# Reordering the lead-in of an attention and feed-forward layer: Q's half rows, the parts' buffers, and V as pieces

## The chip, the core and the metric

The kernel runs on one core of a Trainium2 chip. A core has TensorE (PE, matrix products from SBUF into PSUM), VectorE (DVE), ScalarE (ACT), GpSimd (POOL) and SyncE (SP), which run side by side and wait for each other by semaphores; transfers between HBM and SBUF are issued by an engine's queue (here SP and ACT) and carried by 16 shared DMA engines. The metric is the device time of one execution in microseconds (us), lower is better. Each engine executes its own instructions in the order in which they are written.

## What is computed

One post-norm transformer layer on x of 8 batches x 1024 rows x 256. Attention has 16 heads of width 16 with a fixed additive mask on the distance between query and key; the feed-forward part has ternary weights with a scale and a low-rank addition. Cut to what matters here:

```python
Q = split_heads(x @ Wq.T + bq)
K = split_heads(x @ Wk.T + bk)
V = split_heads(x @ Wv.T + bv)
scores = einsum('bhqd,bhkd->bhqk', Q, K) / sqrt(16)
scores = scores + prior_lambda * gaussian_mask(1024)
attn = softmax(scores, axis=-1)
out = einsum('bhqk,bhkd->bhqd', attn, V)       # heads put together again
x = layernorm(x + out @ Wo.T + bo)
x = layernorm(x + ffn(x))                      # ternary weights, relu squared, low rank
```

## The kernel before

**Parts.** A product in full precision is made of several in a rounded type: Q and K are split into a rounded copy and the rounded difference, and both are kept as the two halves of a tile two. For a chunk of 8 heads (128 rows of Q or K) write_parts (line 190) writes them to HBM in an order of four 16-row layers per head, with two DMAs for K and three for Q per half of 512 columns. fill_stack (line 287) reads them back, four tiles for K and four for Q per group G of 4 heads, as operands stack["k", ...] and stack["q", ...] with 64 rows of layers, 256 KB each. The stack has two slots, so group G + 1 is filled while G is worked on.

**Two passes over the scores.** For every block of 128 queries max_scores (line 636) multiplies Q by K, and max_row (line 658) adds the mask and takes the maximum over 1024 keys in one VectorE instruction of about 1.22 us, whose elementwise result goes to a tile with the tag junk that nobody reads. set_max (line 672) turns the 16 x 128 maxima of one half, negates and splits them, writes them to HBM and reads them back as two extra rows of stack["q"]. exp_scores (line 699) then computes the transposed scores with those rows, so the maximum is subtracted by the product itself; ACT takes the exponential, and weigh (line 749) multiplies by V and by a column of ones.

**The loop.** The loop at line 1462 counts g from -12 (LEAD) to the end. In step g the maxima of item g + 12 are computed and, from g = 0 on, the exponentials of item g; one item is a pair of 128x1024 score blocks for 2 heads. So steps -12 to -1 are the lead-in: maxima alone. PSUM in the loop is three score tiles (se, used in turn), one accumulator (av), and two half banks (misc, used in turn) for everything else. That else is a list of pieces, jobs: products of Q and K for the other 8 heads and for the next batch, turning of x, V, the feed-forward part. A piece issues its matmuls and returns a second function that empties the half bank. In the lead-in, every second step takes one piece from jobs (two at g = -12): the load of x(1, 0) and six of the eight pieces of queries_keys(0, 1).

**Before the loop.** SP loads x's half 0, the biases of K and Q, x's half 1, lambda and bv; ACT issues the loads of the four weights. PE turns the weights and x (128 x 128 transposes), first_part (line 199) makes parts of K half 0, Q half 0, K half 1 and Q half 1 for the first 8 heads. In each, ACT reads the product from PSUM twice (a full copy and the rounded one), VectorE subtracts, and the lower 64 rows (the first 4 heads) are written to HBM at once; the writes of the upper 64 rows are kept in second_heads. Then fill_stack(0) is issued with K on SP's queue and Q on ACT's (line 301), then second_heads, then fill_stack(1) (line 327) and five small loads. Between, PE computes V of batch 0 with 32 records (line 317) and VectorE adds its bias (line 307). The tiles two have the tags two, junk, o0 and o1: buffers that later work uses for other things.

**Order.** At the end of the function all instructions of an engine are chained in written order, so a late operand holds up whatever stands behind it on that engine. A tile that takes over a tag waits until the last reader of the old tile, DMAs included, is done. DMA completions are counted on eight semaphores in rotation, so a DMA also waits for the one issued eight before.

Of the kernel before, what the change touches and what calls it, by code (L numbers as in the profile page):

```python
# [16 lines left out]
P = 128  # L17
HD = 16
# [20 lines left out]
def tile_postln_layer(  # L39
# [60 lines left out]
        x_of[b, half] = t  # L100

    load_x(0, 0)
    raw = {}
    for name, w in (("k", wk), ("q", wq), ("v", wv), ("o", wo)):
        t = big(f"raw_{name}")[:, : NDC * D].rearrange("p (c d) -> p c d", d=D)
# [3 lines left out]
    for name, src in (("k", bk), ("q", bq)):  # L109
        t = cpool.tile([P, NDC], F32, tag=f"b{name}", name=f"b{name}")  # L110
        nc.sync.dma_start(t, src.rearrange("(c p) -> p c", p=P))
        bcol[name] = t
    load_x(0, 1, "hi")
    lam = cpool.tile([P, 1], F32, tag="lam", name="lam")
    nc.sync.dma_start(lam, prior_lambda.partition_broadcast(P))
    bv_row = cpool.tile([P, D], F32, tag="bv_row", name="bv_row")
# [35 lines left out]


    qscale = float(HD) ** -0.5
    nc.vector.tensor_scalar_mul(bcol["q"], bcol["q"], qscale)
    wT = {}

    def turn_weights(name, copy):

        t = cpool.tile([P, NDC, D], F32, tag=f"w{name}T", name=f"w{name}T")  # L160
        pt = bank0(f"pt_{name}")
        for dc in range(NDC):
            for ec in range(NDC):
                at = NDC * dc + ec
                nc.tensor.transpose(pt[:, ts(at, P)], raw[name][:, ec, ts(dc, P)], ident)
        copy(t.rearrange("p c d -> p (c d)"), pt)
        wT[name] = t


    xT = cpool.tile([P, NDC, L], F32, tag="xT", name="xT")  # L170
# [2 lines left out]
    def first_turn(half):  # L173
        xb = x_of.pop((0, half))
        for dc in range(NDC):
            pt = bank0(f"ptx_0_{dc}_{half}")
            for c in range(QB):
                nc.tensor.transpose(pt[:, ts(c, P)], xb[:, c, ts(dc, P)], ident)
            nc.scalar.copy(xT[:, dc, ts(half, HALF)], pt)
        turned[0, half] = 2 * NDC  # L180

    parts_of, made = {}, {}
# [13 lines left out]
            nc.sync.dma_start(to[:, 2, :], two[:, 1, :])  # L196
            nc.sync.dma_start(to[:, 3, :], two[:, 0, :])

    def first_part(name, scale, half, tag, full):
        pt = bank0(f"p{name}_0_0_{half}")  # L200
        for dc in range(NDC):
            nc.tensor.matmul(
                pt,
                wT[name][:, dc, :P],
                xT[:, dc, ts(half, HALF)],
                start=(dc == 0),
                stop=(dc == NDC - 1),
            )
        two = p1.tile([P, 2, HALF], F32R, tag=tag, name=f"two{name}_0_0_{half}")
        for to in (full, two[:, 0, :]):  # L210
            nc.scalar.activation(
                to, pt, AF.Identity, bias=bcol[name][:, 0:1], scale=scale
            )
        nc.vector.tensor_sub(two[:, 1, :], full, two[:, 0, :].bitcast(F32))

        t = parts_of[name, 0, 0]
        write_parts(name, t, two, half, slice(0, P // 2))
        second_heads.append(lambda: write_parts(name, t, two, half, slice(P // 2, P)))

    second_heads = []  # L220
    for name in "kq":
        new_parts(name, 0, 0)
    made[0, 0] = 2 * NHALF
    fulls = [
        p2.tile([P, HALF], F32, tag="rl", name="full_0"),
        p1.tile([P, HALF], F32, tag="avs", name="full_1"),
        p2.tile([P, HALF], F32, tag="r", name="full_2"),
        p2.tile([P, HALF], F32, tag="r", name="full_3"),
    ]
    turn_weights("k", nc.vector.tensor_copy)  # L230
    first_turn(0)
    turn_weights("q", nc.vector.tensor_copy)
    first_part("k", 1.0, 0, "two", fulls[0])
    first_part("q", qscale, 0, "junk", fulls[1])
    first_turn(1)
    first_part("k", 1.0, 1, "o0", fulls[2])
    first_part("q", qscale, 1, "o1", fulls[3])
    turn_weights("v", nc.vector.tensor_copy)
    turn_weights("o", nc.scalar.copy)
    woT = wT["o"]  # L240
# [43 lines left out]
        nc.gpsimd.memset(t[:, :, :, HD : HD + 1], 1.0)  # L284
        v_bufs.append(t)

    def fill_stack(G, queues=(nc.sync, nc.sync)):

        (b, g), s = divmod(G, NG), G % SLOTS
        assert made.get((b, g // 2)) == 2 * NHALF  # L290
        for pr in range(NP):
            for a in range(2):
                at = P // 2 * a
                src = HD * ((g % 2) * HG + 2 * pr + a)
                for name, queue in zip("kq", queues):
                    queue.dma_start(
                        stack[name, s, pr, a][at : at + P // 2].bitcast(F32),
                        parts_of[name, b, g // 2][src : src + HD].rearrange("p l n -> (p l) n"),
                    )

    fill_stack(0, (nc.sync, nc.scalar))
    for write in second_heads:
        write()


    def add_bias(b, t, pv):
        nc.vector.tensor_add(
            v_bufs[b % 2][:, t, :, :HD],
            pv.rearrange("p (h w) -> p h w", w=HD),
            bv_row.rearrange("p (h w) -> p h w", w=HD),  # L310
        )

    for tp in range(NB // 2):
        pv = bank0(f"pv_0_{tp}")
        for i in range(2):
            for dc in range(NDC):
                nc.tensor.matmul(
                    pv[:, ts(i, D)],
                    xT[:, dc, ts(2 * tp + i, P)],
                    wT["v"][:, dc, :],  # L320
                    start=(dc == 0),
                    stop=(dc == NDC - 1),
                )
        for i in range(2):
            add_bias(0, 2 * tp + i, pv[:, ts(i, D)])

    fill_stack(1)
    bo_row = cpool.tile([P, D], F32, tag="bo_row", name="bo_row")
    nc.sync.dma_start(bo_row, bo.partition_broadcast(P))
    gate_c = cpool.tile([P, 1], F32, tag="gate", name="gate_c")  # L330
    nc.sync.dma_start(gate_c, gate.partition_broadcast(P))
    fb_sb = cpool.tile([R, R], F32, tag="fb", name="fb_sb")
    nc.sync.dma_start(fb_sb, fast_b)
    v_sb = p2.tile([R, D], F32, tag="r", name="v_sb")
    nc.sync.dma_start(v_sb, v)
    u_sb = p2.tile([P, NHC, R], F32, tag="r", name="u_sb")
    nc.sync.dma_start(u_sb, u.rearrange("(c p) r -> p c r", p=P))


    before.close()  # L340
# [245 lines left out]
    def queries_keys(b, c, bank):  # L586
# [1 line left out]

        st = {}

        def piece(name, scale, half, k):
            t = new_parts(name, b, c) if half == 0 and k == 0 else parts_of[name, b, c]
            pt = bank(f"p{name}_{b}_{c}_{half}_{k}")
            for dc in range(NDC):
                nc.tensor.matmul(  # L595
                    pt,
                    wT[name][:, dc, ts(c, P)],
                    xT[:, dc, ts(2 * half + k, D)],
                    start=(dc == 0),
                    stop=(dc == NDC - 1),  # L600
                )

            def empty():
                bias = bcol[name][:, c : c + 1]
                if k == 0:
                    st["full"] = p2.tile(
                        [P, HALF], F32, tag="rl", name=f"full{name}_{b}_{c}_{half}"
                    )
                full = st["full"]
                nc.scalar.activation(full[:, ts(k, D)], pt, AF.Identity, bias=bias, scale=scale)  # L610
                if k == 0:
                    return
                two = p1.tile([P, 2, HALF], F32R, tag="two", name=f"two{name}_{b}_{c}_{half}")
                nc.scalar.copy(two[:, 0, :], full)  # L614
                nc.gpsimd.tensor_sub(two[:, 1, :], full, two[:, 0, :].bitcast(F32))  # L615
                made[b, c] = made.get((b, c), 0) + 1
                write_parts(name, t, two, half)

            return empty
# [1 line left out]
        return [  # L621
            (
                0.86,
                lambda name=name, scale=scale, half=half, k=k: piece(name, scale, half, k),
                1,
                lambda half=half: has_xT(b, half),
            )
            for half in range(NHALF)
            for name, scale in (("k", 1.0), ("q", qscale))
            for k in range(2)  # L630
        ]

# [39 lines left out]
    def set_max(step):  # L672
# [6 lines left out]
        def empty():  # L679
# [9 lines left out]
            for j in range(HG):  # L689
                at = 0 if j % 2 else P // 2  # L690
                row = stack["q", s, j // 2, j % 2].bitcast(F32)
                nc.sync.dma_start(row[at : at + 2, ts(h, HALF)], rows[:, j])

        return empty

# [763 lines left out]
    ]  # L1459
    rest, es = None, {}  # L1460
    jobs = [u for part in jobs_of(0) for u in part]
    for g in range(-LEAD, total + 1):

        now = g
        if 0 <= g < total and g % per_batch == 0:
            if g:
                assert not jobs
# [19 lines left out]
            work.append(piece)  # L1487
            halves -= 1

        done = g + LEAD - 2  # L1490
        if done >= 0 and done % QSTEP == QSTEP - 1 and done < total:
            work.append(lambda done=done: set_max(done // QSTEP))
            halves -= 1
        if g < 0:
            if g % 2 == 0:
                work += [jobs.pop(0)[1] for _ in range(2 if g == -LEAD else 1)]
        elif g < total:
            left = per_batch - 1 - g % per_batch
            if g == 0:
# [7 lines left out]
            while jobs and halves >= jobs[0][2] and ready(jobs[0]):  # L1507
# [12 lines left out]
                    break  # L1520
                if jobs and jobs[0][0] > 0.1 and jobs[0][2] == 0:
                    halves = 0
        empties = [piece() for piece in work]
        if g + LEAD < total:
            pair, blk, pm = max_scores(g + LEAD)
            max_row(pair[0], blk, pm[:, 0:1], f"{g + LEAD}_0")
            rest = pair[1], blk, pm[:, 1:2], f"{g + LEAD}_1"
        for empty in empties:
            if empty is not None:
# [82 lines left out]
```

## Time and profile before

| | us |
|---|---|
| median of 3 runs | 2251.11 |
| lowest and highest | 2249.8, 2251.25 |
| the profiled execution | 2246.88 |
| its span, first to last instruction | 2245.1 |

The page's engine rows give busy time, share of the span and instructions; the second block cuts the span into 40 slices of 56 us each, with busy tenths, the granted TensorE clock in tenths, and the GB/s of the transfers:

```
PE 2167.9 (97%) x13144; PEld 1262.1 (56%) x13144; DVE 1591.8 (71%) x2959; ACT 1441.8 (64%) x2152; POOL 893.3 (40%) x1000
PE   6999999999999999999999999999999999999996
DVE  5777777777777776777767777677777777677736
PEclk8899999999999999999999999999999999999998
GB/s 204 91 76 109 59 73 124 90 72 71 100 116 105 37 74 116 131 68 78 69 131 104 73 67 89 131 85 52 74 119 122 78 73 52 139 56 58 23 35 20
```

The first slice is unlike the others: TensorE at six tenths, a clock of 8, and the highest rate of transfers. It holds the part before the loop and most of the lead-in, where the timeline gives 38.34 for the start of the first maximum and 69.58 for the first exp scores.

### The profile page before, as it was taken

How to read it: one execution, taken by the hardware profiler on the slowest of the kernel's cores; microseconds unless marked ns; L12 is line 12 of the kernel's file. 1: busy time of each engine (PE TensorE's matmuls, PEld its weight loads, DVE VectorE, ACT ScalarE, POOL GpSimd, SP SyncE). 2: the span in 40 equal slices, each digit the busy share in tenths (PEclk: the TensorE clock that was granted, in tenths of full speed). 3: DMA queues.
4: the chain of work that ended last, by engine and by line, in shares of the span. 5: the costliest groups of instructions: out<-in, count | busy, mean ns of one | idle time of the engine just before them, and what ended most of it. 6: DMA issues, size and time to landing. Idle time of an engine off the chain costs nothing.

```text
span 2245.1 us, 36797 instructions
## 1 busy us (share of the span) xinstructions
PE 2167.9 (97%) x13144; PEld 1262.1 (56%) x13144; DVE 1591.8 (71%) x2959; ACT 1441.8 (64%) x2152; POOL 893.3 (40%) x1000
## 2 busy tenths in 40 slices
PE   6999999999999999999999999999999999999996
PEld 3444445565555655556555565555555555555556
DVE  5777777777777776777767777677777777677736
ACT  2466556766667667666666667676666666666654
POOL 3023232344324454344532444335443345345443
PEclk8899999999999999999999999999999999999998
DMA  8223233323343124423243223421344321422010
GB/s 204 91 76 109 59 73 124 90 72 71 100 116 105 37 74 116 131 68 78 69 131 104 73 67 89 131 85 52 74 119 122 78 73 52 139 56 58 23 35 20
DMA packets 110189, 193.36 MB, mean 86 GB/s; under 512 B 20973, under 2 KB 49981, under 8 KB 110005
## 3 DMA queue, kind: packets, MB, share of 16 engines
q1 hardware_dynamic: 108596, 188.91, 30.5%
q8 instruction: 104, 1.70, 0.3%
q10 hardware_dynamic: 1408, 2.10, 0.3%
q14 instruction: 81, 0.66, 0.1%
HBM read 105.19 MB, written 85.69 MB: 85 GB/s over the span
## 4 chain that ended last, share of the span: by engine, by line
PE 78%; DVE 8%; POOL 1%; ACT 1%; issue 1%; DMA 1%; SPq 0%; POOLq 0%; DVEq 0%; ACTq 0%
PE e L715 21%; PE av L754 18%; PE s L649 14%; DVE junk L661 5%; PE e L725 5%; PE misc L1028 4%; PE misc L1063 4%; PE misc L595 4%; PE misc L954 2%; PE misc L568 2%; PE misc L1035 1%; ACT exp L739 1%; DVE st L912 1%; PE misc L988 1%; PE misc L542 0%
## 5 line engine op out<-in xcount | busy, mean ns | idle before, releaser
L661 DVE CUSTOM_DVE_ANT_0 junk<-s,wide 128x1024 f32<-128x1024 f32 x1024 | 1248.7, 1219 | 534.7 <-PE s L649 483.7
L739 ACT ACTIVATE exp<-e 128x1024 f32<-128x1024 f32 x1024 | 1027.3, 1024 | 630.3 <-PE e L725 383.1
L715 PE MATMUL e<-st_q,st_k 66*128 66x512 f32 (+1 forms) x2048 | 666.1, 426 | 1.4 <-DVE pm L661 0.9
L715 PEld LDWEIGHTS e<-st_q,st_k 66*128 66x128 f32 (+1 forms) x2048 | 324.6, 189 | 464.4 <-ACT exp L739 81.8
L754 PE MATMUL av<-exp,v 128*17 128x512 f32 x4096 | 540.5, 599 | 0.0
L649 PE MATMUL s<-st_k,st_q 64*128 64x512 f32 x2048 | 403.6, 449 | 43.0 <-DVE pm L661 33.2
L649 PEld LDWEIGHTS s<-st_k,st_q 64*128 64x128 f32 x2048 | 168.1, 186 | 182.5 <-DVE pm L661 78.0
L738 DVE TENSOR_TENSOR e<-e,wide 128x372 f32<-128x372 f32 (+2 forms) x376 | 190.8, 508 | 53.9 <-PE e L715 48.6
L1046 POOL TENSOR_TENSOR rl<-rl 128x512 f32<-128x512 f32 x112 | 116.7, 1042 | 250.2 <-ACT hi L1045 243.7
L725 PEld LDWEIGHTS e<-prior,ident_r 128*128 128x128 f32 x1056 | 160.3, 190 | 24.3
L754 PEld LDWEIGHTS av<-exp,v 128*17 128x17 f32 x4096 | 68.0, 95 | 185.8 <-issue 183.1
L725 PE MATMUL e<-prior,ident_r 128*128 128x244 f32 (+2 forms) x1056 | 158.2, 272 | 0.0
L1048 POOL TENSOR_TENSOR lo<-rl,hi 128x512 fp32r<-128x512 f32 x112 | 145.4, 1298 | 8.8
L1083 POOL TENSOR_TENSOR r<-r,sp_row 128x256 f32<-128x256 f32 x56 | 41.1, 734 | 203.7 <-ACT r L1082 203.5
L578 POOL TENSOR_TENSOR v<-v,bv_row 128x256 f32<-128x256 f32 x56 | 38.5, 687 | 195.8 <-ACT v L577 195.8
L1028 PE MATMUL misc<-xhi,wfT 128*128 128x256 f32 x448 | 116.0, 282 | 0.2 <-ACT fullq L610 0.2
L1028 PE MATMUL misc<-xlo,wfT 128*128 128x256 f32 x448 | 115.1, 280 | 0.0
L1063 PE MATMUL misc<-wpT,lo 128*128 128x256 f32 x448 | 111.8, 283 | 2.1 <-POOL lo L1048 2.1
L1063 PE MATMUL misc<-wpT,hi 128*128 128x256 f32 x448 | 113.8, 287 | 0.0
L615 POOL TENSOR_TENSOR twok<-fullk,twok 128x512 fp32r<-128x512 f32 x30 | 39.0, 1300 | 187.1 <-ACT twok L614 187.1
L1041 ACT ACTIVATE rl<-misc,s_fc 128x256 f32<-128x256 f32 x224 | 94.1, 475 | 0.1
L1063 PEld LDWEIGHTS misc<-wpT,lo 128*128 128x128 f32 x448 | 85.0, 190 | 6.3 <-POOL lo L1048 2.9
(235 smaller groups left out, 2348.8 us busy)
## 6 DMA issues: line engine op xcount, KB each, us to landing
st_k<-parts_k SPq DMA_DIRECT2D x128, 256.0 KB
st_q<-parts_q SPq DMA_DIRECT2D x124, 256.0 KB
parts_k<-twok SPq DMA_DIRECT2D x60, 512.0 KB
parts_q<-twoq SPq DMA_DIRECT2D x64, 256.0 KB
parts_q<-twoq SPq DMA_DIRECT2D x30, 512.0 KB
x<-in_L_attn_x_dram SPq DMA_DIRECT2D x16, 512.0 KB
raw_o<-avs SPq DMA_DIRECT2D x248, 32.0 KB
rec<-back SPq DMA_DIRECT2D x30, 256.0 KB
```

The costliest lines, as they stand in the source:

```text
L649: nc.tensor.matmul(pair[a][:, kh, :], stack["q", s, pr, a][rows, ts(blk, P)], stack["k", s, pr, a][rows, ts(kh, HALF)], start=True, stop=True,
L661: nc.vector.tensor_tensor_reduce(out=junk, in0=t.rearrange("p k n -> p (k n)"), in1=wide[:, LEFT - P * blk : LEFT - P * blk + L], scale=1. ...
L715: nc.tensor.matmul(t[:, a, :], stack["k", s, pr, a][rows, ts(blk, P)], stack["q", s, pr, a][rows, ts(h, HALF)], start=True, stop=not by_pe,)
L725: nc.tensor.matmul(t[:, a, lo - HALF * h : hi - HALF * h], ident_r, prior[:, n, lo - first : hi - first], start=False, stop=(n == 1),)
L738: nc.vector.tensor_add(part, part, add.to_broadcast([P, 2, hi - lo]))
L739: nc.scalar.activation(e, t.rearrange("p a n -> p (a n)"), AF.Exp)
L754: nc.tensor.matmul(av[32 * j : 32 * j + HD + 1, :], v_bufs[b % 2][:, blk, g * HG + j, : HD + 1], es[j // 2][:, ts(j % 2, HALF)], start=(n ...
L1028: nc.tensor.matmul(ph, wfT[:, dc, ts(hc, P)], st[k2][:, dc, :], start=(dc == 0 and k2 == "xhi"), stop=False,)
L1041: nc.scalar.activation(rl[:, ts(k, n)], ph, AF.Relu, scale=s_fc[:, hc : hc + 1])
L1046: nc.gpsimd.tensor_mul(rl, rl, rl)
L1048: sub(lo, rl, hi.bitcast(F32))
L1063: nc.tensor.matmul(py, st[k][:, hc, ts(i, P)], wpT[:, hc, :], start=(hc == 0 and k == "hi"), stop=(hc == NHC - 1 and k == "lo"),)
```

## The change

Before the loop:

- x's half 1 is loaded straight behind half 0, ahead of the biases.
- The factor 1/4 of the scores is put into Q's turned weights and bias, not into every activation.
- A part is one ACT pass (the rounded copy, with bias) and one VectorE pass that takes product + bias - rounded copy straight from PSUM. The full copies are gone. Of the four copies of x's turned blocks the last goes to VectorE.
- Order: K half 0, turning of x half 1, Q half 0, K half 1, Q half 1. Q half 0 is held in a buffer of the exponentials (tag e) and no longer in junk.
- Of Q only half 0 of the lower rows is written before the fills. K's four fills go to SP, four half fills of Q (512 columns) to ACT; then SP writes Q half 1 lower rows, all upper rows, and fills the second halves of Q.
- V is no longer computed here. fill_stack(1) and the five small loads move into step g = -2.

In the lead-in: 14 pieces, V and Q/K in turn, are spread over the steps, placed behind the step's scores rather than ahead; the step of set_max (now g = -4) takes none. The load of x(1, 0) is left in jobs and comes at g = 0. In set_max of the first half two of the four reads are issued by ACT.

```diff
     load_x(0, 0)
+    load_x(0, 1, "hi")
...
-        copy(t.rearrange("p c d -> p (c d)"), pt)
-        wT[name] = t
+        t = t.rearrange("p c d -> p (c d)")
+        if name == "q":
+            nc.vector.tensor_scalar_mul(t, pt, qscale)
+            nc.vector.tensor_scalar_mul(bcol["q"], bcol["q"], qscale)
+        else:
+            copy(t, pt)
...
-            nc.scalar.copy(xT[:, dc, ts(half, HALF)], pt)
+            copy = nc.vector.tensor_copy if dc == half == 1 else nc.scalar.copy
+            copy(xT[:, dc, ts(half, HALF)], pt)
...
-        two = p1.tile([P, 2, HALF], F32R, tag=tag, name=f"two{name}_0_0_{half}")
-        for to in (full, two[:, 0, :]):
-            nc.scalar.activation(
-                to, pt, AF.Identity, bias=bcol[name][:, 0:1], scale=scale
-            )
-        nc.vector.tensor_sub(two[:, 1, :], full, two[:, 0, :].bitcast(F32))
...
+        nc.scalar.activation(two[:, 0, :], pt, AF.Identity, bias=bias)
+        nc.vector.scalar_tensor_tensor(
+            out=two[:, 1, :],
+            in0=pt,
+            scalar=bias,
+            in1=two[:, 0, :].bitcast(F32),
+            op0=ALU.add,
+            op1=ALU.subtract,
+        )
+        return two
...
-    first_part("k", 1.0, 0, "two", fulls[0])
-    first_part("q", qscale, 0, "junk", fulls[1])
+    two["k", 0] = first_part("k", 0, two_tile("k", 0, p1, "two"))
+    write_parts("k", parts_of["k", 0, 0], two["k", 0], 0, low)
     first_turn(1)
-    first_part("k", 1.0, 1, "o0", fulls[2])
-    first_part("q", qscale, 1, "o1", fulls[3])
+    two["q", 0] = first_part("q", 0, two_tile("q", 0, epool, "e"))
+    write_parts("q", parts_of["q", 0, 0], two["q", 0], 0, low)
+    two["k", 1] = first_part("k", 1, two_tile("k", 1, p1, "o0"))
+    write_parts("k", parts_of["k", 0, 0], two["k", 1], 1, low)
+    two["q", 1] = first_part("q", 1, two_tile("q", 1, p1, "o1"))
...
-    fill_stack(0, (nc.sync, nc.scalar))
-    for write in second_heads:
-        write()
...
+    halves_of_q = slice(0, HALF), slice(HALF, L)
+    for pr in range(NP):
+        for a in range(2):
+            fill_one("k", 0, pr, a, nc.sync)
+            fill_one("q", 0, pr, a, nc.scalar, halves_of_q[0])
+    write_parts("q", parts_of["q", 0, 0], two["q", 1], 1, low)
+    for (name, half), t in two.items():
+        write_parts(name, parts_of[name, 0, 0], t, half, high)
+    for pr in range(NP):
+        for a in range(2):
+            fill_one("q", 0, pr, a, nc.sync, halves_of_q[1])
...
+                queue = nc.scalar if step == 0 and j % 2 else nc.sync
+                queue.dma_start(row[at : at + 2, ts(h, HALF)], rows[:, j])
...
+    v_first, qk_first, jobs[:7] = values(0, misc), jobs[1:7], jobs[:1]
+    early = [u for two in zip(v_first, qk_first) for u in two] + v_first[6:]
     for g in range(-LEAD, total + 1):
...
+        if g == -2:
+            fill_stack(1)
+            load_later()
...
-        done = g + LEAD - 2
+        done = g + LEAD - (1 if g < 0 else 2)
...
         if g < 0:
-            if g % 2 == 0:
-                work += [jobs.pop(0)[1] for _ in range(2 if g == -LEAD else 1)]
+
+            n = g + LEAD + 1 - (done >= QSTEP - 1)
+            upto = 14 * n // (LEAD - 1)
+            if halves == 2:
+                work += [early.pop(0)[1] for _ in range(len(early) - 14 + upto)]
...
-        empties = [piece() for piece in work]
+        empties = [piece() for piece in work] if g >= 0 else []
         if g + LEAD < total:
             pair, blk, pm = max_scores(g + LEAD)
             max_row(pair[0], blk, pm[:, 0:1], f"{g + LEAD}_0")
+            if g < 0:
+
+                empties = [piece() for piece in work]
```

fill_one is the body of the old fill_stack for one tile, with a choice of columns; load_later holds the five small loads; low and high are the lower and upper 64 rows; values is the function that makes V's pieces for the later batches (ACT copies the product, POOL adds the bias).

## The prediction

> **What bounds the kernel now.** I read the chain of waits first, by engine, then the timeline of the first 95 us, then windows over them.
>
> ```profile
> PE 78%; DVE 8%; POOL 1%; ACT 1%; issue 1%; DMA 1%; SPq 0%; POOLq 0%; DVEq 0%; ACTq 0%
> ```
>
> TensorE sets the end over most of the span, and the change leaves its work the same: the change can only move the moment at which the steady loop (g = 0, the first exp scores, line 715) begins. So the question is what sets that moment. The timeline, with the lines that matter (start, duration, engine, line, operation, idle before it and what ended that):
>
> ```profile
> 13.56 0.71 SPq L192 DMA_DIRECT2D parts_k<-twok  x1
> ...
> 19.73 0.61 SPq L194 DMA_DIRECT2D parts_k<-twok  x1
> ...
> 23.75 2.51 SPq L296 DMA_DIRECT2D st_k<-parts_k  x4
> ...
> 26.41 2.85 ACTq L296 DMA_DIRECT2D st_q<-parts_q  x4
> ...
> 33.48 0.73 PE L649 MATMUL s<-st_k,st_q 64*128 64x512 f32 x4 [0.47 <-DMA st_q<-parts_q]
> 33.70 1.57 SPq L197 DMA_DIRECT2D parts_q<-twoq  x1
> ...
> 38.34 1.23 DVE L661 CUSTOM_DVE_ANT_0 junk<-s,wide 128x1024 f32<-128x1024 f32 x1 [8.20 <-DMA parts_q<-twoq]
> ...
> 69.58 1.19 PE L715 MATMUL e<-st_q,st_k 66*128 66x512 f32 x2 [0.33 <-issue]
> ```
>
> Read it so: parts of K and Q go to HBM from 13.56 on, come back as the stacked operands from 23.75 on, the first scores stand at about 34.0, but the first maximum starts at 38.34. It waited for a write of parts of Q: its output tile has the tag junk, which still holds Q's parts of half 0 (second_heads writes them out again at 32.43 to 35.27). From there the maxima set the pace, and the windows show it:
>
> ```profile
> 15.00:25.00 10.00, 8.14 (x33) 5.53 (x34) 4.79 (x12) 3.49 (x6) 4.33 (x7) 1.00 0.91 196
> 25.00:34.00 9.00, 5.70 (x26) 4.00 (x24) 2.75 (x7) 0.47 (x1) 0.00 (x0) 1.00 1.04 270
> ```
> ```profile
> 38.34:69.47 31.13, 22.93 (x64) 11.01 (x64) 27.11 (x44) 4.64 (x10) 4.28 (x4) 0.72 0.74 195
> ```
> ```profile
> 40.00:42.00 2.00, 2.00 (x6) 1.17 (x5) 1.86 (x3) 0.00 (x0) 0.00 (x0) 0.50 0.92 201
> ...
> 46.00:48.00 2.00, 1.54 (x6) 0.84 (x5) 1.86 (x4) 0.47 (x1) 0.00 (x0) 1.00 1.06 231
> ```
>
> Columns: stretch, length, busy time of PE, PEld, DVE, ACT, POOL, then granted clock, DMA share, GB/s. The transfers are full from 15 to 34 (0.91 and 1.04). From 38.34 to 69.47 VectorE does 22 maxima (44 instructions with their read-outs) in 31.13, 1.415 each; an undisturbed pair starts 1.38 after the last (38.34, 39.72, 41.09), so 22 x 1.38 = 30.4 and 0.8 is lost to late scores. TensorE is idle often enough to be granted half its clock for 19 us of these (34.6 to 44.4, 50.7 to 61).
>
> **The change, part by part.**
>
> *Parts (lines 199 to 237).* One ACT pass and one VectorE pass straight from PSUM replace two ACT passes and a subtraction. For K half 0 the product ends at 11.50; ACT 0.68 (row L211) to 12.2, VectorE 0.69 (row L214, SBUF) to 0.76 (row L738, PSUM, 0.55 for 372 columns, scaled to 512) to 12.95. The first write is issued near 13.0, not 13.56: 0.55 earlier. Then x's half 1 is turned ahead of Q: 8 transposes 1.04 to 12.45, Q's product 1.88 to 14.3, ACT to 15.0, difference to 15.75; Q's three writes take 0.57 + 1.05 + 1.23 = 2.85 of issue, 15.8 to 18.65 (before 15.28 to 18.22, so later by 0.4). K half 1 queues behind them on SP: 18.65 to 19.9 (0.45 earlier than 20.34). x's half 1 is there: transfers stand still from 10 to 14. The other removed work (two ACT passes of 0.68, one bias scaling of 0.44 that is only moved) lies beside the transfers and is worth nothing else; without that cover it would be 1.4.
>
> *Order of the fills.* The three blocks that the first scores need (K both halves, Q half 0) are 3 x 0.52 MB; at 196 GB/s 8.0 us, from 14.5: all written by 22.5. Before, the fourth block (Q half 1, 20.80 to 23.64) went ahead of the K fills. Now ACT issues four half fills of Q (0.52 MB) as soon as Q half 0 has landed, near 21, which flow from about 22.5, and K's fills follow when K half 1 has landed, 23 to 24.3 (0.7 later for what it shares). Data begin 1.5 after issue (13.56 to 15). The first two K fills are 0.52 MB and 0.4 MB of Q's is left beside them: 0.92 MB at 270 GB/s is 3.4. So 23.6 + 1.5 + 3.4 = 28.5, plus 0.9 for a pair of scores and a completion of 0.4: the first maximum at 29.8. Bounds: 28 (no sharing) and 31.5 (all at 200 GB/s).
>
> [...]
>
> *The tile of Q's half 0* moves from tag junk to the tag e. The wait of the first maximum, 38.34 - 34.0 = 4.3, goes, and is contained in the 38.34 - 29.8 = 8.5 gained there. Tag e is used next by the exponentials at g = 0, when the second writes are 20 us old. Tag two (K half 0) is next wanted by the cast at g = -9, near 39; its second write is fifth in a queue of 2.1 MB and lands near 35. No new wait.
>
> *V as pieces.* Out of the gap before the scores go 32 matmuls (21.43 to 28.60) and 8 bias additions on VectorE; both lay beside the transfers and their removal is worth 0. Into the twelve groups of maxima go 8 pieces, each TensorE 4 records (row L595: 1.10 at full clock, 2.08 at half), ACT 0.37 (row L577), POOL 0.69 (row L578). Each group then has 4 score matmuls (0.245 each at full clock, 0.43 at half) and on average 14/12 pieces, against 6/12. At full clock that is 0.98 + 1.28 = 2.26, under VectorE's 2.76: hidden. At half clock it is 1.72 + 2.43 = 4.15: not hidden. Which clock holds is the main unknown. TensorE will now be idle from about 19.6 to 28, longer than the idle stretch after which the clock fell (34.6), so the lead-in starts at half. In the trace it rose at 44.2, 4.8 after TensorE became busy throughout at 39.4. Two groups of 1.72 + 2.08 = 3.8 lie in 4.8 + 2.8, a loss of 2 x 1.05 = 2.1. After that the pieces keep TensorE at 0.75 to 0.85 of VectorE's time; in 46 to 50, at 0.7, the full clock lasted 6.5. Three groups with two pieces (g = -9, -5, -1) need 0.98 + 2.20 = 3.2, 0.4 over each. Loss taken: 2.1 + 1.2 - 0.8 (the loss of before) = 2.5, bounds 0 and 5. Where TensorE is warm at g = 0, the first step of the loop (5.7 before, at 0.5 to 0.7 of the clock, against 4.0 to 4.6 in the next two) gives back 1; bounds 0 and 1.7.
>
> [...]
>
> *Moved transfers.* fill_stack(1), five small loads and the load of x(1, 0) go behind the lead-in's writes. SP order at g = -6 to 3: parts of chunk 1, rows of maxima, 8 fills (2.1 MB), five loads, K parts (1.05 MB), x (0.52 MB). The fills issue at about 58; 2.1 MB at 235 GB/s end near 68.5, wanted at g = 4 (near 78). K parts and x, at 350 GB/s (full-height writes before: 408 in 56 to 58), land near 73.5; x is first turned at g = 3, near 75. Taken at 0; bounds 0 and 4, since the margin is 1.5. The rows of maxima: set_max moves up to g = -4, near 54.5; sub, write, and read before took 69.5 - 61.3 at most; they land by 61, wanted at 63. ACT issues two of the reads and stands in its queue till the rows are written (2.5, row L686 to L692); behind it is a V copy whose half bank is wanted two groups later. Taken at 0, bounds 0 and 1.5.
>
> *Sum.* First exp scores at 29.8 + 31.1 + 2.5 - 0.4 (scores with V behind them, not before) = 63.0 against 69.58: 6.6 earlier, and 1 in the first step: 7.6. The profiled execution took 2246.88 (span 2245.1 and 1.8 around it); 7.6 off gives 2239.3. It ran 4.2 below the median of the three runs, 2251.11; carried to that: 2243.5. Ends: 28 and no loss, 1.7 back: 12, 2239; 31.5, loss 4, x late by 1: 2.5, 2248.5.
>
> **Rivals.**
>
> *TensorE at half clock takes VectorE's place (slower).* If the clock stays at 0.5 through the twelve groups, the lead-in takes 48 x 0.43 + 14 x 2.08 + 0.4 = 50.1. From 29.8 the loop starts at 80, 10.4 late: 2261.5. It decides from a lead-in of 39.8 on, that is half clock in about half of the twelve groups. For it: half clock in 19 of 31 us before. Against it: then TensorE is never idle, and in this trace that has always brought the clock back within 5 us.
>
> *The gain is given back to a late transfer.* x or the rows come 3 to 4 late: 2247. For it: a margin of 1.5; 10 MB must pass from 26 on, 50 us at 200 GB/s. Against it: SP takes them in order, and only the fill of G = 1 is new ahead of x.
>
> *It moves only the junk wait.* If K's fills are no earlier (sharing takes all of it), the first maximum comes at 34.0; 4.3 less 2.5, plus 1: 2.8, 2248.3. For it: transfers already full. Against it: 0.52 MB less goes ahead of the fills.
>
> **How the numbers follow.** The forecast has 0.68, the half clock 0.08, the late transfer 0.14, only the junk wait 0.10. About 0.2%, 4.5 us, is what a measurement of this kernel can tell from no change, so faster begins below 2246.6. The forecast gives 0.66 of faster and 0.02 of same; the late transfer 0.05 and 0.09; the junk case 0.03 and 0.07; the half clock 0.08 slower. In sum 0.74, 0.18, 0.08. The range 2239 to 2248.5 holds the forecast and most of the two middle cases.
>
> **What would show it.** The first maximum at 28 to 31.5 with TensorE, not a DMA of parts, as its releaser; 22 maxima in 31 to 36 us with granted clock above 0.72; exp scores from 59 to 66; no wait for x at the first turn of x(1, 0); the same spacing from g = 4 on. Wrong it would be if the clock stays at 0.5 past 45, or if the first maximum comes after 34.

## The result and the profile after

| | before | changed |
|---|---|---|
| median, us | 2250.79 (4 runs, 2249.80 to 2251.25) | 2236.41 (4 runs, 2234.14 to 2239.97) |
| the profiled execution, span | 2246.88, 2245.1 | 2234.62, 2232.8 |

The ratio is 0.9934, 95% interval 0.9920 to 0.9948: 14.4 us faster, by the interval 11.7 to 18.0. The forecast was 7.6 us. Its direction held and its size did not: 2236.41 lies below the range of 2239 to 2248.5.

The chain of waits after, by engine:

```profile
PE 81%; DVE 9%; issue 1%; POOL 1%; ACT 1%; DMA 1%; SPq 0%; POOLq 0%; DVEq 0%; ACTq 0%
```

TensorE has a larger share of a shorter span, so waits went and not work. The timeline after, with the lines that answer to those shown of before:

```profile
12.15 0.71 SPq L196 DMA_DIRECT2D parts_k<-twok  x1
...
14.74 0.57 SPq L196 DMA_DIRECT2D parts_q<-twoq  x1
...
16.01 0.79 SPq L201 DMA_DIRECT2D parts_q<-twoq  x1
16.90 0.60 SPq L196 DMA_DIRECT2D parts_k<-twok  x1
17.54 0.61 SPq L198 DMA_DIRECT2D parts_k<-twok  x1
...
19.32 2.74 ACTq L298 DMA_DIRECT2D st_q<-parts_q  x4
...
22.02 2.41 SPq L298 DMA_DIRECT2D st_k<-parts_k  x4
...
27.04 1.19 PE L647 MATMUL s<-st_k,st_q 64*128 64x512 f32 x3 [0.42 <-DMA st_k<-parts_k]
27.87 1.22 DVE L659 CUSTOM_DVE_ANT_0 junk<-s,wide 128x1024 f32<-128x1024 f32 x1 [6.44 <-PE s L647]
...
61.00 0.81 PE L714 MATMUL e<-st_q,st_k 66*128 66x512 f32 x2
```

The first maximum waits for scores and no longer for a write of Q's parts, and the scores wait for K's fill, which is now the last to land. Five landmarks carry the whole comparison. Each kernel was profiled a second time, unedited:

| landmark, us | before | before again | changed | changed again |
|---|---|---|---|---|
| first maximum | 38.34 | 37.84 | 27.87 | 28.03 |
| first exp scores | 69.58 | 68.72 | 61.00 | 61.48 |
| exp scores of the next step | 75.23 | 74.11 | 64.43 | 64.91 |
| first accumulator copied | 106.75 | 105.63 | 95.38 | 95.88 |
| end of span | 2245.1 | 2244.3 | 2232.8 | 2234.4 |

By the means of the two columns the lead is 10.1 at the first maximum, 7.9 at the exp scores, 10.0 one step later, 10.6 at the accumulator and 11.1 at the end. So the lead-in gave back 2.2 of what was won ahead of it, and 2.7 came back from there to the first accumulator. Windows over both, before and after (columns as in the prediction):

```profile
69.60:106.80 37.20, 35.85 (x184) 18.97 (x185) 26.98 (x48) 21.23 (x29) 1.75 (x2) 0.93 0.18 64
```
```profile
27.87:61.00 33.13, 29.73 (x102) 17.17 (x102) 28.83 (x47) 7.17 (x17) 8.34 (x10) 0.83 0.71 199
61.00:95.40 34.40, 32.86 (x184) 16.86 (x183) 25.16 (x45) 21.39 (x30) 3.05 (x4) 1.00 0.44 123
```

The same 184 matmul records take 37.20 before and 34.40 after; the granted clock is 0.93 before and 1.00 after. In the lead-in the clock is 0.83 (0.72 before), and V's pieces are in TensorE's 29.73. Windows of 2 us say where the clock was halved. Before, half clock lay from 34.2 to 44.4, from 51.3 to 61.5 and from 68.3 to 75.2, so 5.6 us of it fell behind the first exp scores (5.0 in the second trace). After, it lay from 22.2 to 32.4 and from 52.9 to 59.7, and none behind the first exp scores. The first line is of before, the others of after:

```profile
70.00:72.00 2.00, 2.00 (x8) 1.71 (x8) 1.86 (x3) 0.40 (x1) 0.00 (x0) 0.50 0.76 285
```
```profile
28.00:30.00 2.00, 2.00 (x5) 1.17 (x4) 1.86 (x3) 0.00 (x0) 0.00 (x0) 0.50 1.04 374
54.00:56.00 2.00, 2.00 (x7) 0.90 (x5) 1.86 (x4) 0.37 (x1) 0.69 (x1) 0.50 0.36 76
62.00:64.00 2.00, 1.80 (x9) 0.77 (x7) 0.65 (x2) 1.72 (x3) 1.17 (x2) 1.00 1.07 223
```

### The profile page after: what moved, and what is told of

It reads as the page before. It is cut to its first block, busy times and chain, and to the rows that moved or that the text cites. A ratio compares the mean times of both kernels' runs of the same rounds, so it can differ in the third digit from the quotient of the medians.

```text
span 2232.8 us, 36805 instructions
## 1 busy us (share of the span) xinstructions
PE 2160.5 (97%) x13144; PEld 1259.3 (56%) x13144; DVE 1589.8 (71%) x2952; ACT 1442.6 (65%) x2155; POOL 895.5 (40%) x1008
## 3 DMA queue, kind: packets, MB, share of 16 engines
q1 hardware_dynamic: 108908, 189.42, 30.9%
## 4 chain that ended last, share of the span: by engine, by line
PE 81%; DVE 9%; issue 1%; POOL 1%; ACT 1%; DMA 1%; SPq 0%; POOLq 0%; DVEq 0%; ACTq 0%
PE e L714 22%; PE av L753 19%; PE s L647 15%; DVE junk L659 6%; PE e L724 5%; PE misc L1027 4%; PE misc L593 4%; PE misc L1062 4%; PE misc L953 2%; PE misc L566 2%; PE misc L1034 1%; DVE st L911 1%; PE misc L987 1%; ACT exp L738 1%; DMA rows<-both 0%
## 5 line engine op out<-in xcount | busy, mean ns | idle before, releaser
L576 POOL TENSOR_TENSOR v<-v,bv_row 128x256 f32<-128x256 f32 x64 | 43.8, 686 | 212.6 <-ACT v L575 212.6
```

## The experiments

All start from the changed kernel unless said otherwise; landmarks are those of the table.

**Q's half 0 in junk again.**

```diff
-    two["q", 0] = first_part("q", 0, two_tile("q", 0, epool, "e"))
+    two["q", 0] = first_part("q", 0, two_tile("q", 0, p1, "junk"))
```

> The changed kernel with Q's half 0 back in the tile tagged junk. Theory (the output tile of the maxima holds the first one up until Q's upper rows are written): the second writes of Q's half 0 are issued at 28.0 to 31.8 in the changed kernel and land some 2 later, so the first maximum starts at 33.5 to 34.5 with a DMA of Q's parts as its releaser, not at 27.9; exp scores near 66.5, time 5 to 6 us more. Rival (the scores are what is late, the tile only shows as the last waiter): the first maximum stays within 0.5 of 27.9 and the time within 1 us.

```profile
33.72 1.23 DVE L659 CUSTOM_DVE_ANT_0 junk<-s,wide 128x1024 f32<-128x1024 f32 x1 [12.27 <-DMA parts_q<-twoq]
```

The maximum again waits for a write of Q's parts, 5.8 later, with scores ready at about 28. Exp scores at 64.96, 4.0 later and not 5.5: the lead-in ran in 31.2 in place of 33.1. Scores lay ready when it began, and by 2 us windows only 5.4 us of it were at half clock, in place of 11.4; the run does not part the two. Time 2242.54. The tile is shown to be a wait of its own.

**The tile alone, in the kernel before.** The same exchange of tags in the old first_part.

> The kernel before with one part of the change alone: Q's half 0 in a buffer with the tag e in place of junk. Theory (that tile held the first maximum up by the 4.3 between 34.0 and 38.34): first maximum at 34.0 to 34.5 released by scores, exp scores 65.3 to 66.5 in place of 69.6, time 3 to 4.5 us less than before. Rival (the wait is replaced by another write that the maxima wait for): first maximum at 37 or later.

```profile
33.98 1.23 DVE L661 CUSTOM_DVE_ANT_0 junk<-s,wide 128x1024 f32<-128x1024 f32 x1 [4.33 <-PE s L649]
```

First maximum at 33.98, released by scores; exp scores 65.50; accumulator 102.35; time 2245.18. So this one part alone is worth 4.1 at the first maximum and 3.8 at the accumulator (means of before). The rest, 6.0 at the first maximum, is from all other parts together: the fills' order, the parts' passes, the order of x and the bias.

**All four blocks ahead of the fills.**

```diff
+    write_parts("q", parts_of["q", 0, 0], two["q", 1], 1, low)
     turn_weights("v", nc.vector.tensor_copy)
...
-            fill_one("q", 0, pr, a, nc.scalar, halves_of_q[0])
+            fill_one("q", 0, pr, a, nc.scalar)
```

(The later write of this block and the second half fills are gone with it.)

> The changed kernel with all four blocks of the lower rows written before the fills, and Q filled whole. Theory (volume ahead of K's fills): 0.52 MB more at 200 GB/s, 2.6 us, and 0.52 MB more of Q's fills shared with K's, about 1: the first maximum at 31 to 32, exp scores 3 to 4 later than 61.0. Rival (the order of issue is hidden behind the landing of K's half 1): first maximum at most 28.5.

```profile
32.88 1.22 PE L647 MATMUL s<-st_k,st_q 64*128 64x512 f32 x3 [0.70 <-DMA st_q<-parts_q]
33.72 1.22 DVE L659 CUSTOM_DVE_ANT_0 junk<-s,wide 128x1024 f32<-128x1024 f32 x1 [11.77 <-PE s L647]
```

First maximum at 33.72, released by scores that waited for a fill of Q; K's fills at 22.91. That is 5.8 later, where 3 to 4 was expected: Q's fills are not issued before 25.54, and each is twice as long. About 0.5 of the 5.8 is none of this: K's first product took 2.69 in this run (1.88 and 2.18 in the two traces of the changed kernel). Exp scores 65.67, time 2243.49. Undone alone, the order of the fills costs as much at the first maximum as the junk tile did. The two do not add up, since 5.8 and 5.8 are more than the 10.1 that the whole change brings there: where one is missing, it hides part of the other.

**V ahead of the loop again.** The block of V from before put back (32 matmuls, bias on VectorE), six pieces in the lead-in.

> The changed kernel with V computed ahead of the loop again (32 matmuls, bias on VectorE), only six pieces of Q and K in the lead-in, behind the scores. Theory (TensorE's idle stretch from 17.5 to 25.9 costs the clock, and the pieces then wait at half clock): full clock from 26 to 33, lead-in 31 to 31.5 in place of 33.1, first maximum at 27.9 to 28.4, exp scores at 59 to 59.8, time 1 to 2 us less than the changed kernel. Rival (V's pieces are hidden beside the maxima and V ahead of the scores delays them): first maximum later by 0.5 or more, exp scores at 61 or later, time the same or more.

First maximum 28.28, lead-in 32.5, exp scores 60.74, accumulator 96.24; median 2236.95, ratio 0.9937 (0.9923 to 0.9952), which is the changed kernel's. The clock stayed at 1.00 to 28 and 0.95 from 28 to 30, but fell later, and for longer:

```profile
28.00:30.00 2.00, 0.91 (x7) 0.36 (x5) 1.57 (x3) 0.00 (x0) 0.00 (x0) 0.95 1.00 322
30.00:32.00 2.00, 2.00 (x7) 1.17 (x4) 1.86 (x3) 0.00 (x0) 0.00 (x0) 0.50 1.03 320
40.00:42.00 2.00, 0.99 (x3) 0.50 (x3) 1.86 (x3) 0.00 (x0) 0.00 (x0) 0.51 0.93 278
58.00:60.00 2.00, 2.00 (x6) 1.00 (x6) 1.67 (x3) 0.47 (x1) 0.00 (x0) 0.50 0.67 186
```

From 40.0 to 60.5 the granted clock is at half; with six pieces TensorE was busy for 1.06 of 2.00 from 38 to 40, ahead of the fall, and for 0.99 from 40 to 42. A second thing went against this run: its first turn of x waited for the load, which was issued at 69.78 (66.51 in the changed kernel, which has no such wait):

```profile
74.82 0.41 PE L561 MATMUL misc<-ident,x 128*128 128x128 f32 x2 [1.26 <-DMA x<-in_L_attn_x_dram]
```

So the equal median covers opposite terms: exp scores 0.3 to 0.7 earlier, and 1.26 for x behind them. V as pieces shows no worth of its own on the time. What the windows show is where half clock lay: with V as pieces from 22.2 to 32.4 and not from 34 to 52 (1.00), with V ahead from 29.8 to 33.2 and from 40.0 to 60.5.

**Transposes that nobody reads, to keep the clock.**

```diff
+    warm = bank0("warm")
+    for i in range(56):
+        nc.tensor.transpose(warm[:, ts(i % 4, P)], ident, ident)
```

> The changed kernel with 56 more 128x128 transposes of the identity, read by nobody, between the turning of the weights and the first scores (17.5 to 25). Theory (the idle stretch costs the clock, and the first groups then run at half): full clock till 33 at least, lead-in 31.2 to 32 in place of 33.1 to 33.4, exp scores 59 to 60, time 1 to 2 us less than the changed kernel. Rival (the clock in the lead-in costs nothing at the end): exp scores at 61 or later, or the same time.

They ran from 17.59 to 23.87, and the first scores came at 26.85; the clock stood at 1.00 to 26 and at 0.57 from 26 to 28. Exp scores 61.14, lead-in 32.35. Median 2234.70 (2232.34 to 2235.07), ratio 0.9936 (0.9919 to 0.9952): not to be told from the changed kernel. The theory was tested in part only: half clock lay from 26.3 to 33.1 and from 53.6 to 57.0, so 7.7 us of it fell into the lead-in in place of 11.4 and 12.0, and the lead-in was 0.8 and 1.1 shorter. The later first maximum (28.79) took this back.

**Four of V's blocks ahead, 30 transposes behind them, ten pieces.**

> The changed kernel with four of V's eight blocks computed ahead of the loop, then 30 transposes of the identity that nobody reads, and ten pieces in the lead-in. Theory (TensorE busy until 25.5 keeps the clock, and four pieces fewer leave room): full clock till 33 or longer, first maximum at 27.8 to 28.3, lead-in 30.8 to 31.8, exp scores at 58.8 to 60, time 1 to 2 us below the changed kernel. Rival (the clock falls a few us later for the same length, as in the two runs with V or transposes there): exp scores at 60.5 or later, time the same within 1.

Here the clock held to 30 (0.97 from 28 to 30): first maximum 27.78, lead-in 31.0, exp scores 58.77, 2.5 earlier than the mean of the changed kernel. It is no test of the clock alone: four pieces are gone from the lead-in, and the clock was at half in it for 10.3 us (29.9 to 33.3, 50.4 to 57.2), nearly as long as in the changed kernel. What half clock costs the lead-in is better read from nine traces that all have 14 pieces there: with 5.4 to 7.7 us of half clock it took 31.2 to 32.4, with 11.4 to 12.0 it took 33.1 to 33.5. That is about 0.25 for each us, and so about 3 in the changed kernel, an estimate. And the earlier exp scores came to nothing: median 2237.37 (ratio 0.9955, 0.9938 to 0.9971), accumulator at 100.62. The waits of TensorE from 58 to 100:

```profile
PE misc L564 <- DMA x<-in_L_attn_x_dram: 3.1, 1, 3.1
```

x of the next batch was issued at 71.68, since fewer pieces per step pushed the parts of Q, and the fills behind them, back (56.90 and 58.71); and the clock fell twice more, 64.0 to 67.4 and 77.7 to 81.1. The rival of the late transfer is real, one step beyond the changed kernel.

**The load of x at the first step.**

```diff
-    v_first, qk_first, jobs[:7] = values(0, misc), jobs[1:7], jobs[:1]
+    v_first, qk_first = values(0, misc), jobs[1:7]
+    jobs[0][1]()
+    jobs[:7] = []
```

> The changed kernel with the load of x of the next batch issued at the first step of the lead-in, as before the change, and no longer at g = 0. Theory (in the changed kernel x lands just in time, so its place costs nothing there): exp scores within 0.7 of 61.0 to 61.5, the copy of the first accumulator at 95 to 96, the time within 2 us of 2236.6. Rival (x is late by 1 or more): the copy of the first accumulator at 94.5 or earlier and the time lower by 1 to 2.

Exp scores 61.57, as expected; but the accumulator at 97.02, 1.1 to 1.6 later than in the changed kernel, and the median 2241.11 (ratio 0.9965, 0.9952 to 0.9979), 4.5 above the mean of the changed kernel's two medians. Both theories fall. No wait for x is there in either kernel; with the load gone from the list, every later piece starts one step sooner. First this run, then the changed kernel:

```profile
66.71 1.02 PE L593 MATMUL misc<-xT,wqT 128*128 128x256 f32 x4
70.81 0.38 PE L540 MATMUL misc<-ident,x 128*128 128x128 f32 x2
```
```profile
69.85 1.02 PE L593 MATMUL misc<-xT,wqT 128*128 128x256 f32 x4
73.50 0.38 PE L540 MATMUL misc<-ident,x 128*128 128x128 f32 x2
```

From the first exp scores to the accumulator it took 35.45. The changed kernel, with no half clock there either, took 34.38 and 34.40, and three of the other edits, with none, 34.36, 34.39 and 34.64. So about 1.05 is lost there, and not by the clock. The load, left in the list as an entry of its own, moved batch 0's pieces by a step, and this place is better. The run moved the DMA as well as the pieces: that the pieces are the cause is argued, that the edit costs this much is shown. The rest of the 4.5 comes behind the accumulator, and no run here says where.

**All of it together**: four blocks ahead, 30 transposes, x first, Q and K ahead of V in the list.

> The changed kernel with four of V's blocks ahead of the loop, 30 transposes of the identity that nobody reads, the load of x in the first step of the lead-in, and the pieces of Q and K ahead of V's. Theory (the earlier exp scores of the run with four blocks ahead were lost to a late x and to parts of Q behind which the fills stood): exp scores at 58.5 to 59.5, no wait for x, the copy of the first accumulator at 92.5 to 94.5, the time 1.5 to 2.5 us below the changed kernel, near 2234.5. Rival (another wait takes its place, or half clock comes later): the copy of the first accumulator at 95 or later, the time the same within 1.

Exp scores 60.46, accumulator 98.28, median 2240.92 (ratio 0.9963, 0.9949 to 0.9977): slower than the changed kernel. It has the load's place of the run before, and half clock from 49.1 to 59.3 and, behind the exp scores, from 73.0 to 76.4; what each of them costs here was not parted. No version that was tried is shown to beat the changed one.

**The bias scaling, both ways.** In the changed kernel, put back ahead of the copies:

> The changed kernel with the scaling of Q's bias put back ahead of the copies of the turned weights on VectorE. Theory (K's first product waits for K's turned weights, which wait behind the scaling, which waits for the bias to land; in the changed kernel that is near 9.8): K's turned weights copied near 10.3 in place of 6.6, first write of K's parts at 13.8 to 14.6 in place of 12.2 to 12.4, fills of K and first maximum 1.5 to 2.3 later than 27.9. Rival (the scaling lies beside the transfers, as the prediction had it): first maximum within 0.4 of 27.9.

```profile
9.70 0.55 DVE L155 TENSOR_SCALAR bq<-bq 128x2 f32<-128x2 f32 x1 [3.81 <-DMA bq<-in_L_attn_bq_dram]
9.78 0.68 DVE L170 COPY wkT<-pt_k 128x512 f32<-128x512 f32 x1
```

K's turned weights 3.2 later (6.60 in the changed kernel), first write 15.67, first maximum 31.54, accumulator 99.63: 3.6 at the first maximum, more than the 1.5 to 2.3 expected. K's first product started 1.9 later than in the changed kernel (10.61, and 8.73 there), which is the scaling and as expected; it then took 3.53 in place of 1.88, which is not (see the next run but one). With x ahead of the biases this move is needed. In the kernel before, moved behind:

> The kernel before with one part of the change alone: the scaling of Q's bias moved behind the copies of the turned weights of K and Q on VectorE. Theory (it held K's turned weights, and so K's first product, up): the first write of K's parts at 11.9 to 12.7 in place of 12.7 to 13.6, K half 1's write 0.5 to 0.9 earlier, the first maximum 0.3 to 0.9 earlier than 37.8 to 38.3, since Q's second writes, which it waits for, stand behind the same transfers. Rival (beside the transfers): no landmark moves by more than the 0.6 by which two traces of before differ.

First write 12.57 (12.71 and 13.56 in two traces of before), first maximum 37.85, within what these span; time 2249.80. There the bias landed at 7.9, and K's first product waited for x's turned block, copied until 8.77, and not for the weights, copied until 7.99. So the rival, at the first maximum: beside the transfers in the old order, on the path in the new one. One landmark does not keep to the rival's 0.6: the accumulator, at 107.94, is 1.2 later than the later of before, in a run with half clock from 70.0 to 80.3, for which the edit gives no reason.

**x's half 1 behind the biases.**

> The changed kernel with x's half 1 loaded behind the biases again. Theory (the biases wait behind 0.5 MB of x and nothing on the path needs them before 10): the first write of K's parts within 0.3 of 12.2, K half 1's write 0 to 0.6 later, first maximum 27.8 to 28.6. Rival (x's half 1 is what K half 1 and Q half 0 wait for, so that its early load is worth 1 or more): first maximum at 28.9 or later.

First write 13.26, first maximum 29.37, accumulator 97.28, time 2237.69. This fits the rival's number, but the trace gives another place for it: K's first product took 3.11 here, and 1.88 and 2.18 in the two traces of the changed kernel; 0.9 to 1.2 of the 1.4 is that. The four matmuls waited for nothing that the profile shows, and the windows give a granted clock of 1.00 for each us from 6 to 12 in both; TensorE was slow for longer. First this run, then the changed kernel:

```profile
8.61 3.11 PE L206 MATMUL pk<-xT,wkT 128*128 128x512 f32 x4
9.47 0.34 PEld L206 LDWEIGHTS pk<-xT,wkT 128*128 128x128 f32 x1 [0.52 <-issue]
```
```profile
8.73 1.88 PE L206 MATMUL pk<-xT,wkT 128*128 128x512 f32 x4
9.16 0.19 PEld L206 LDWEIGHTS pk<-xT,wkT 128*128 128x128 f32 x1 [0.24 <-ACT xT L183]
```

In the lead-in four weight loads of this size took 0.29 to 0.34 at a granted clock of 0.50 (from 40.8 to 42.1 in the kernel before), and 0.19 on average at 1.00 (34 to 52 in the changed kernel). The same product took 2.68 and 1.98 in the two traces of before. Whether x's place has a part in this is open; the exp scores, at 61.28, were no later than in the changed kernel.

**Two passes per part.**

> The changed kernel with the parts made by two ACT passes and a subtraction, as before. Theory (a pass of 0.69 on ACT lies on the path of every part, and ACT's queue carries it on to K half 1): the first write of K's parts 0.6 later, K half 1's write 0.6 to 1.5 later, the first maximum 0.6 to 1.5 later than 27.9. Rival (all beside the transfers): first maximum within 0.4.

First write 13.30, K half 1 at 18.07, first maximum 29.13, accumulator 96.94, time 2239.49. Of the 1.2 at the first maximum 0.5 is the pass (2.05 from the end of K's first product to the first write, 1.54 in both traces of the changed kernel), and most of the rest is that product, 2.38 this time. One copy and one difference is worth about 0.5 here.

**The two kernels again.**

> The changed kernel again, nothing edited, to see how far its executions differ. First maximum within 0.3 of 27.9. Theory (stretches of half clock that come in some executions and not in others make the spread): time between 2234 and 2240, exp scores within 1.5 of 61.0, and a lower mean clock in the longer runs. Rival (the transfers make it): first maximum moves by more than 1.

> The kernel before again, nothing edited, for a second trace. Theory (what differs between executions is when TensorE falls to half clock): first maximum within 0.4 of 38.3, the first 12 groups in 31 to 32, half clock in the first steps of the loop again, the copy of the first accumulator within 1 of 106.75, and a different place or count of short stretches of half clock later, worth up to 4. Rival (the transfers of the lead-in vary): the first maximum differs by more than 1.

The changed kernel came out as expected. Before missed three of its numbers narrowly: the first maximum is 0.5 off where 0.4 was given, the 12 groups took 30.9 where 31 was the least, and the accumulator is 1.1 off where 1 was given. The changed kernel's median was 2236.83 (2235.52 to 2237.50), ratio 0.9939 (0.9922 to 0.9955).

Between 100 and 2100 us every trace, of before and after alike, has one to three more stretches at half clock, at 164 to 208, at 348 to 362 or near 1940, most of them 3.4 long. Such a stretch costs about 1.6, an estimate: from the first exp scores to the accumulator three edits of the changed kernel with one of them took 35.95 to 36.0, three with none 34.36 to 34.64. They go with the largest moves of the lead between the first two traces, which runs between 11.4 and 14.0 from one accumulator to the next; not every move is explained. Over all sixteen traces the time from the first accumulator to the end lies between 2135.1 and 2141.6, so a difference of a few us between two single traces, at the end, says little.

## Why the prediction was right or wrong

- *What bounds it.* Right: the lead at the start is carried to the end (10.6 at the first accumulator, 11.1 at the end, means of two traces).
- *The junk wait, 4.3.* Right: 4.1 alone (before) and 5.8 undone (changed).
- *The first maximum at 29.8.* Too late by 1.9; within its bounds of 28 to 31.5 but for 0.1. The term that failed is the write of K half 1, put at 18.65 to 19.9 and issued at 16.90 to 18.15. Half of it: K's first product was taken from one execution, 2.68 long, while over all runs it took 1.9 to 3.5, by how long TensorE stayed slow at the start; that it took 1.88 in the profiled run is luck, not the change. The other half: Q's three writes, 2.85 of issue by their rows of before, were done in 2.06 (14.74 to 16.80), at a DMA share of 0.94 where before had 0.92; why they were shorter was not shown. From K's fills on, the working held: 5.0 from issue to the scores, 4.9 forecast. From there to the first maximum 0.83 was measured (27.04 to 27.87), where 0.9 and 0.4 for a completion were taken; no run shows the 0.4 by itself.
- *The bias scaling, "only moved", worth nothing else.* In the old order that is what it is worth at the first maximum; in the new one the move is worth about 1.9 (of the 3.6 in the run that undid it the rest is the slow product), because x goes ahead of the biases. The price should have been put on the order that the change makes.
- *V as pieces and the clock.* The lead-in took 33.13 and was put at 33.2. The number is right in part by luck: half clock lay from 22.2 to 32.4 and from 52.9 to 59.7, where one stretch, at the start, was forecast, and the second lies where the prediction counted on pieces to keep the clock. Ahead of it is the step of set_max, which takes no piece: its scores alone left TensorE busy for 2.08 of 3.40 from 49.5 to 52.9. By the experiments such half clock costs about 3 in the lead-in, near the 2.5 taken. The reading of before was a little off as well: half clock lay at 34.2 to 44.4 and 51.3 to 61.5, and 0.72 over 31.13 makes 17 us of it, not 19.
- *The return of the clock, 4.8.* It was read at one place of one trace. In the changed kernel the clock came back 5.4 after TensorE was last idle (27.04 to 32.4) and 6.0 in its second trace (27.20 to 33.2), in the kernel before 4.8 (39.6 to 44.4) and 3.9 in its second trace (39.1 to 43.0). Nor was it always back within 5 us in the trace that the prediction read: at the first step of the loop TensorE was busy from 69.58 and the clock rose at 75.2, 5.6 later.
- *First step of the loop, 1.* It gave 2.1 (5.65 and 5.39 before, 3.43 and 3.43 after), beyond the bound of 1.7: TensorE entered the loop at full clock and kept it (1.00 from 61.00 to 95.40). The term was mis-sized: the 5.6 and 5.0 us of half clock that before has behind the first exp scores went whole, and 2.7 came back by the first accumulator, not 1. Three edits that also had no half clock there took 34.36 to 34.64 from the exp scores to the accumulator, as the changed kernel did (34.4).
- *Moved transfers, taken at 0, bounds 0 and 4.* The step with the wrong sign. x was not late in the changed kernel, so 0 was right for the transfer. But the load is an entry of the list as well, and leaving it there moved batch 0's pieces a step later; undoing that costs about 1.05 between the exp scores and the first accumulator and 4.5 in the median. The bounds allowed a loss only, and no reason had excluded a gain.
- *The sum.* 6.6 forecast at the exp scores, 7.9 measured; then 1 forecast, 2.7 measured by the first accumulator. The lower end of the range had failed by its own terms: 28 with no loss and 1.7 given back makes 12.6 and not 12, so 2238.5; the time measured lies below that too. The medians differ by 14.4, the spans of the traces by 9.9 to 12.3, so 2.1 to 4.5 of the 14.4 is not in the traces. Of this, 1.8 is the choice of runs: over all 34 timed runs of before, here and beside the experiments, the median is 2249.4, and over 8 of the changed kernel 2236.8, a difference of 12.6. Why single runs of before differ by up to 7 stays open.
- *Rivals.* Half clock did not decide the lead-in. The late transfer was absent here but took 1.26 in the run with V ahead of the loop and 3.1 in the run with exp scores at 58.77. That only the junk wait moves is excluded by 27.87.

## What to carry to other kernels

A start-up is priced on the order that the change makes: an edit that is free in the old order (the bias scaling) can be what lets another edit work. An entry of a paced list is not free because its work is: moving it shifts every later piece, and the bounds of such a move need both signs. A landmark taken from one trace carries that trace's own luck; two traces of the kernel before would have shown that the first product differs by 0.7 from run to run. The same holds for an experiment: the run that undid the bias move reads 3.6 as a landmark, and 1.9 once the part that only this execution had is taken off.

## What was not expected of the hardware

TensorE's clock fell without a long pause. In the run with V ahead of the loop, with scores in each group of 2.8 us, TensorE was busy for 1.11, 1.46 and 1.06 of 2.00 from 34 to 40, and from 40 to 42 it was granted 0.51; with a piece in nearly every group, as changed, it was busy for 14.60 of 18.00 from 34 to 52 and granted 1.00. The last 6.9 us ahead of the changed kernel's fall at 52.9 read (0.86 busy, then 0.61):

```profile
46.00:49.50 3.50, 3.02 (x14) 2.17 (x15) 3.07 (x7) 0.98 (x4) 1.28 (x1) 1.00 0.14 56
49.50:52.90 3.40, 2.08 (x10) 0.84 (x8) 3.11 (x5) 0.84 (x4) 1.12 (x2) 1.00 0.66 253
```

In the kernel before TensorE was busy for 1.19, 1.22 and 1.37 of the 3.40 ahead of its three falls at 34.2, 51.3 and 68.3. No busy share that decides a fall is shown: 2.17 of 3.40, from 122.9 to 126.3 in the kernel before, was followed by full clock, and in the run with x's half 1 behind the biases the clock fell near 65.7 after 1.87 of 2.00 from 62 to 64. The stretches of half clock below 100 us were 10.2, 10.2 and 6.8 long in the kernel before, 10.2 and 6.8 in the changed kernel, 6.8 and 3.4 (53.6 to 57.0) in the run with 56 transposes, 3.4 and 20.5 (40.0 to 60.5) with V ahead of the loop.

The first matmuls ran at about half the speed of later ones, and the column of the granted clock does not show it: eight transposes took 1.91 from 6.36 on and 1.04 from 10.45 on in the changed kernel, 1.91 from 6.23 on and 1.04 from 13.05 on in the kernel before, at a granted clock of 1.00 in the windows from 6 to 12. How long this lasted differed from run to run, and with it K's first product: 1.88 in the changed kernel, 2.38 with two passes per part, 2.68 in the kernel before, 3.11 with x's half 1 behind the biases.
